# Moving the PSUM evacuations of the second attention layer behind the second exponential of a step on ScalarE

## The chip, the cores and the metric

The kernel runs on one core of one Trainium2 chip. The metric is device time in microseconds (us), the median of the runs shown. Five engines work side by side, each through its own instructions in order: PE (TensorE, matmuls; PEld is its loading of weights), DVE (VectorE), ACT (ScalarE), POOL (GpSimd) and SP (SyncE, which here only issues DMAs). They meet at semaphores. Matmuls write PSUM, and ACT or DVE carry the results from there to SBUF; that carrying is called evacuation below.

## What is computed

Four layers in float32 on x of shape (4, 1024, 256), each added to x after a layer norm: attention A (16 heads of 64), a feed-forward block (256 to 1024 to 256 with gelu), attention B, and the feed-forward block again. Cut to what matters, the third layer is:

```python
h = layernorm(layernorm(x)) * ln_scale + ln_bias
c_q, c_kv = h @ w_down_q.T, h @ w_down_kv.T          # 128 wide each
q, k, v = (c @ w_up.T for ...)                        # 16 heads of 64
q, k = rope(q), rope(k)
attn = softmax(q @ k.T / 8)
x = x + (attn @ v).reshape(b, s, 1024) @ w_out.T
```

## The kernel before, in words

The order of the work is written out by hand: each engine runs its instructions as the Python code issues them. An attention layer walks over 32 groups (four batches, eight pairs of heads) and over eight steps in each, 256 steps in all; a step is 128 query rows of one pair, 64 rows of each of two 64-row blocks, for both heads. `steps_with` (L339) is the loop over steps s. In step s it issues, for the step ahead, `scores(s+1)` (L247, PE, 16 matmul instructions into two tiles `sc`, one for each head), the negated maximum of each tile (L258, DVE), and two exponentials (L260, ACT, `exponentials(s+1, 0)` and `(s+1, 1)`). DVE then transposes the 32x32 squares of step s (L280), SP and POOL send the pieces to other partitions by DMA (L304), and ACT copies one piece (L296). Before that, `invert(s)` takes the reciprocal of the sums (L268, DVE) and copies it out (L269, ACT).

Two steps make one group of 128 query rows, h, five steps later (LAG): in a step with `part == 0`, called a *weighing step* here, PE multiplies the probabilities with v (`weigh`, L313, 128 matmul instructions, into two PSUM banks); ACT copies the two results (L323) and POOL scales them (L325). In the next step, `part == 1`, called a *projecting step* here, PE multiplies with the output weights (`project`, L176 with `wo,oT`), ACT evacuates (L335, `got`) and POOL adds to x (L337).

The work that prepares coming pairs is a table of pieces, each a step and a function. `(s - EARLY)` pieces stand between the two exponentials of step s, `s` pieces at its end. For attention B, `pair_b` gives for each pair two halves of q and k (`qk`: matmul and evacuation, L860), their rotation (`change` L865, `rotate` L870 to L872, a step and two steps later) and two halves of v (`values`, L881). They fall on projecting steps. In each pair two of the four projecting steps get one such piece, and two get two. `batch_b` adds for each coming batch, on some projecting steps that have one: four turnings of the normalized rows (`transposed`, L162 on PE, L167 on ACT) and four products with the down weights (`down`, L835).

PSUM has eight banks of 512 floats. The scores hold six of them: three tiles of two banks, taken in turn. All other results share the last two, which `group` hands out in turn:

```python
    def group(*shape):
        last[0] ^= 1
        return ps_mm.tile([P, *shape], F32, tag=f"m{last[0]}", name="mm")
```

So each new result waits until the one before the last has been evacuated, and the two banks of `weigh` are the banks that the projecting step before it used last. In a projecting step of attention B, ACT's order before the change is: `got` (L335), first exponential, evacuations of the pieces, second exponential. A projecting step with one piece takes two groups there, one with two pieces takes three.

Of the kernel before, what the change touches and what calls it, by code (L numbers as in the profile page):

```python
# [9 lines left out]
F32 = mybir.dt.float32  # L10
# [23 lines left out]
NK2 = S // DH  # L34
EPS = 1e-5
EARLY = 0.5
PLACES = {
    (3, 0): (0, 1), (3, 10): (2,), (3, 11): (3,), (3, 12): (4,), (3, 13): (5,),
    (3, 14): (6,), (3, 15): (7,), (3, 17): (8,), (3, 18): (9,), (3, 19): (14,), (3, 20): (15,),
    (4, 0): (16,), (4, 2): (10, 17), (4, 4): (18,), (4, 6): (19,), (4, 8): (20,), (4, 10): (21,),  # L40
    (4, 14): (11,), (4, 15): (22,), (5, 2): (12,), (5, 14): (13,), (5, 15): (23,),
    (6, 2): (26,), (6, 5): (27,), (6, 8): (28,), (6, 14): (24,), (6, 15): (25,),
    (7, 2): (29,), (7, 4): (30,), (7, 7): (31,), (7, 9): (32,), (7, 11): (33,), (7, 14): (38, 34),
    (7, 15): (35,), (7, 16): (39,), (7, 17): (36,), (7, 19): (37,),
}


# [1 line left out]
def hybrid_block_kernel(  # L49
# [137 lines left out]
                    start=(i == 0), stop=(i == len(parts) - 1),  # L187
                )

    def attention(prep_batch, prep_pair, wo, loader, lead, kept):  # L190

# [133 lines left out]
        def project(h):  # L327
            g, t0 = divmod(HB * h, NT)
            b, pr = pairs[g]
            po = group(HB, D)  # L330
            for t in range(HB):
                paired(po[:, t, :], [(oT[h][:, t], [wos[g][:, t]] * 2)])
            oT.pop(h)
            got = tmp.tile([P, HB, D], F32, tag="tmp", name="got")
            nc.scalar.copy(got, po)  # L335
            xd = xs[b][:, t0 : t0 + HB, :]
            nc.gpsimd.tensor_add(xd, xd, got)  # L337

        def steps_with(others):  # L339
            for k, f in others:  # L340
                pieces.setdefault(k, []).append(f)
            for s in range(-1, n + LAG + 1):
                h, part = divmod(s - LAG, HB)
                ahead = 0 <= s + 1 < n
                if 0 <= s < n:
                    invert(s)
                if ahead:
                    scores(s + 1)
                if part == 1 and 0 <= s // HB - 1 < n // HB:
                    send(s // HB - 1, nc.gpsimd, sent[len(sent) - POOL_DMA :])  # L350
                if part == 1 and 0 <= h < n // HB:
                    project(h)
                if ahead:
                    exponentials(s + 1, 0)
                for f in pieces.get(s - EARLY, ()):
                    f()
                if part == 0 and 0 <= h < n // HB:
                    weigh(h)
                if ahead:
                    exponentials(s + 1, 1)  # L360
                if part == 0 and 0 <= h < n // HB:
                    take(h)
                if 0 <= s < n:
                    turn(s)
                if part == 0 and 0 <= s // HB - 1 < n // HB:
                    keep(s // HB - 1)
                    T.pop(s // HB - 1)
                if part == 0 and 0 <= s < n:
                    send(s // HB, nc.sync, sent[: len(sent) - POOL_DMA])
                for f in pieces.get(s, ()):  # L370
                    f()
# [333 lines left out]
    def layer_a():  # L705
# [5 lines left out]
        def batch_a(b):  # L711
            work = []
            for qb in range(NQB):
                k = {}

                def straight(t, b=b, k=k, qb=qb):
                    if t == 0:
                        k["xn"] = xnp.tile([P, TQ, D], F32, tag="xn", name="xn")
                    dst, src = k["xn"][:, t, :], xs[b][:, qb * TQ + t, :]
                    shift, rstd = rows.factors(NQB * b + qb, t)[:2]  # L720
                    if b == 0 and qb == 1:
                        nc.vector.tensor_scalar(dst, src, rstd, shift, op0=ALU.mult, op1=ALU.add)
                    else:
                        standardize(dst, src, shift, rstd)

                def turned(c, b=b, k=k, qb=qb):
                    if c == 0:
                        p, tag = ((lowp, "low"), (highp, f"high{b % 2}"))[qb]
                        hTs[b, qb] = p.tile([P, NC, QB], F32, tag=tag, name="hT")
                    transposed(hTs[b, qb], k["xn"], c)  # L730

                work += [(10 * qb + t, lambda t=t, f=straight: f(t)) for t in range(TQ)]
                work += [(10 * qb + 6 + 2 * c, lambda c=c, f=turned: f(c)) for c in range(NC)]
            return work

        def pair_a(b, pr):
# [38 lines left out]

        later = [(4 + i, lambda i=i: rows.measure(2 + i // TQ, i % TQ)) for i in range(6 * TQ)]
        later += [(4 + 6 * TQ, lambda: rows.finish[2]())]
        first, steps = attention(batch_a, pair_a, wo_a, nc.gpsimd, lead=3, kept=0)
        loads, xn, pair = first[:2], first[2:14], first[14:]

        def measured(qb):
# [15 lines left out]
    def layer_b(rows):  # L797
# [4 lines left out]
        def batch_b(b):  # L802
            work = []
            for qb in range(NQB):
                k = {}

                def first(t, b=b, k=k, qb=qb):
                    if t == 0:
                        if b:
                            k["x1"] = xnp.tile([P, TQ, D], F32, tag="xn", name="x1")  # L810
                        else:
                            k["x1"] = vp.tile([P, NK2, DH], F32, tag="v", name="x1").rearrange(
                                "p k d -> p (k d)"
                            ).rearrange("p (t d) -> p t d", t=TQ)
                    xt = xs[b][:, qb * TQ + t, :]
                    standardize(k["x1"][:, t, :], xt, *rows.factors(NQB * b + qb, t)[:2])
                    nc.gpsimd.tensor_add(xt, xt, k["x1"][:, t, :])

                def second(t, b=b, k=k, qb=qb):
                    x1 = k["x1"][:, t, :]  # L820
                    nc.scalar.mul(x1, x1, rows.factors(NQB * b + qb, t)[2])

                def turned(c, b=b, k=k, qb=qb):
                    if c == 0:
                        p, tag = (highp, f"high{qb}") if b % 2 == 0 else (lowp, "low")
                        cs[b, qb] = p.tile([P, NC, QB], F32, tag=tag, name="hc")
                    transposed(cs[b, qb], k["x1"], c, affine=(lns_sb, lnb_sb))

                def down(m, b=b, qb=qb):

                    h = cs[b, qb][:, :, ts(m, QB // 2)]
                    pc = group(2, QB // 2)
                    for i in range(2):
                        paired(pc[:, i], [(wd_sb[:, i, c, :], [h[:, c]] * 2) for c in range(NC)])
                    nc.scalar.copy(h, pc)  # L835

                work += [(16 * qb - 14 + t, lambda t=t, f=first: f(t)) for t in range(TQ)]
                work += [(16 * qb - 12 + t, lambda t=t, f=second: f(t)) for t in range(TQ)]
                work += [(16 * qb - 8 + 2 * c - EARLY, lambda c=c, f=turned: f(c)) for c in range(NC)]
                work += [(16 * qb + 2 * m, lambda m=m, f=down: f(m)) for m in range(2)]  # L840
            return work

        def pair_b(b, pr):
# [6 lines left out]

            def qk(i, qb):

                pq = group(QB)
                paired(pq, [(made["w"][:, i, :], [cs[b, qb][:, i]] * 2)])
                name = ("qT", "kT")[i]
                if qb == 0:
                    made[name] = qkp.tile([P, S], F32, tag=name, name=name)
                straight = made[name][:, ts(qb, QB)]
                made[i, qb] = straight
                nc.scalar.mul(straight, pq, (scale_b, 1.0)[i])  # L860
# [13 lines left out]
            def values(qb):  # L874
                if qb == 0:
                    made["v"] = vp.tile([P, NK2, DH], F32, tag="v", name="v")
                pv = group(NK2 // NQB, DH)
                for t in range(NK2 // NQB):
                    lhsT = cs[b, qb][:, 1, ts(t, DH)]
                    by_head(pv[:, t, :], [(lhsT, made["w"][:, 2, :])])  # L880
                nc.scalar.copy(made["v"][:, ts(qb, NK2 // NQB), :], pv)  # L881

            work = []
            for i in (1, 0):
                for qb in range(NQB):
                    k = 2 - 4 * i + 2 * qb
                    work += [(k - EARLY, lambda i=i, qb=qb: qk(i, qb))]
                    work += [(k + 1, lambda i=i, qb=qb: change(i, qb))]
                    work += [(k + 2, lambda i=i, qb=qb: rotate(i, qb))]
            work += [(4 + 2 * qb - EARLY, lambda qb=qb: values(qb)) for qb in range(NQB)]  # L890
            return {name: lambda name=name: made[name] for name in ("qT", "kT", "v")}, load, work

        return attention(batch_b, pair_b, wo_b, nc.sync, lead=5, kept=1)


    n_steps = B * NF * NT
# [72 lines left out]
```

## Time and profile before

| what | value |
|---|---|
| median of 3 runs | 3253.63 us (3250.37 to 3256.33) |
| profiled execution | 3250.15 us |
| its span in the profile | 3248.4 us |
| busy over the span | PE 97%, PEld 64%, DVE 84%, ACT 66%, POOL 62% |
| granted TensorE clock | 0.996 |
| first to last transpose (L280) of attention B | 1671.8 to 3014.2 us |

Four stages follow one another: attention A up to about 1420 us, a feed-forward block up to about 1670, attention B up to about 3010, and the last feed-forward block. In attention B, from 2200 to 2400 us, PE is busy for 198.82 of 200 us, DVE 184.56, POOL 181.85 and ACT 155.75; the DMA engines have a busy share of 0.89.

The profile's tables are read like this. A line of the timeline has the start, the duration, the engine, the source line, the operation, output and inputs, the shapes and the count of merged instructions; in brackets stands the idle time before it and what ended it. A line of the waits has who waited for whom, the sum in us, the number of times and the longest.

### The profile page before, as it was taken

How to read it: one execution, taken by the hardware profiler on the slowest of the kernel's cores; microseconds unless marked ns; L12 is line 12 of the kernel's file. 1: busy time of each engine (PE TensorE's matmuls, PEld its weight loads, DVE VectorE, ACT ScalarE, POOL GpSimd, SP SyncE). 2: the span in 40 equal slices, each digit the busy share in tenths (PEclk: the TensorE clock that was granted, in tenths of full speed). 3: DMA queues.
4: the chain of work that ended last, by engine and by line, in shares of the span. 5: the costliest groups of instructions: out<-in, count | busy, mean ns of one | idle time of the engine just before them, and what ended most of it. 6: DMA issues, size and time to landing. Idle time of an engine off the chain costs nothing.

```text
span 3248.4 us, 128967 instructions
## 1 busy us (share of the span) xinstructions
PE 3164.4 (97%) x53648; PEld 2092.2 (64%) x53648; DVE 2723.5 (84%) x2686; ACT 2137.9 (66%) x4400; POOL 2002.1 (62%) x2782
## 2 busy tenths in 40 slices
PE   8999999999999999999999999999999999999999
PEld 4666666666666666668866566666666666655688
DVE  7988888888888888966569989998999999999554
ACT  5666666666666666655447777777778777777542
POOL 4544545455444545442249889899899889886311
PEclk9999999999999999999999999999999999999999
DMA  8888888888888888850029889988989899988200
GB/s 228 217 224 215 224 224 228 217 219 222 221 217 225 219 231 223 221 150 1 4 74 244 225 228 243 242 237 236 246 243 243 234 240 246 238 235 221 57 20 27
DMA packets 244709, 642.29 MB, mean 198 GB/s; under 512 B 74304, under 2 KB 102976, under 8 KB 244128
## 3 DMA queue, kind: packets, MB, share of 16 engines
q1 hardware_dynamic: 161104, 397.60, 48.0%
q0 software_dynamic: 83024, 236.44, 26.0%
q8 instruction: 426, 6.98, 1.0%
q14 instruction: 155, 1.27, 0.1%
HBM read 43.39 MB, written 4.19 MB: 15 GB/s over the span
## 4 chain that ended last, share of the span: by engine, by line
PE 69%; SPq 12%; DMA 6%; DVE 5%; ACT 4%; issue 3%; POOL 1%; DVEq 0%; ACTq 0%; POOLq 0%
PE sc L247 20%; PE mm L313 19%; PE mm L176 15%; SPq L304 11%; DMA pT<-T 5%; PE pw L495 4%; PE mm L185 4%; PE mm L495 3%; PE mm L615 2%; DVE T L280 2%; DVE nmax L258 1%; ACT p L260 1%; PE ph L604 1%; ACT gT L529 1%; PE mm L162 1%
## 5 line engine op out<-in xcount | busy, mean ns | idle before, releaser
L258 DVE TENSOR_REDUCE nmax<-sc 128x1 f32<-128x1024 f32 x1024 | 1204.5, 1218 | 214.3 <-PE sc L247 211.3
L260 ACT ACTIVATE p<-sc,nmax 128x1024 f32<-128x1024 f32 x1024 | 1145.3, 1119 | 322.3 <-DVE nmax L258 322.2
L280 DVE STREAM_TRANSPOSE T<-p 128x2176 f32<-128x2176 f32 x512 | 1247.3, 2436 | 48.4 <-DMA pT<-T 18.4
L247 PE MATMUL sc<-kT,qT 64*64 64x512 f32 x8192 | 1082.5, 598 | 11.9 <-ACT p L260 10.3
L313 PEld LDWEIGHTS mm<-pT,v 64*64 64x64 f32 x32768 | 949.5, 133 | 140.7 <-issue 98.5
L313 PE MATMUL mm<-pT,v 64*64 64x128 f32 x32768 | 983.0, 269 | 9.6 <-issue 8.5
L304 POOL DMA_DIRECT2D pT<-T x1280 | 629.6, 499 | 125.5 <-PE sc L247 57.7
L325 POOL TENSOR_TENSOR oT<-oT,pT 128x256 f32<-128x256 f32 x256 | 187.0, 730 | 696.3 <-ACT oT L323 623.0
L247 PEld LDWEIGHTS sc<-kT,qT 64*64 64x64 f32 x8192 | 332.8, 133 | 401.6 <-issue 274.5
L337 POOL TENSOR_TENSOR x<-x,got 128x512 f32<-128x512 f32 x256 | 331.0, 1293 | 25.8 <-ACT got L335 22.0
L335 ACT COPY got<-mm 128x512 f32<-128x512 f32 x256 | 150.0, 586 | 281.8 <-PE mm L176 281.8
L176 PE MATMUL mm<-wo,oT 128*64 128x256 f32 x2048 | 279.9, 394 | 24.1 <-POOL oT L325 22.8
L176 PEld LDWEIGHTS mm<-wo,oT 128*64 128x64 f32 x2048 | 124.9, 136 | 273.2 <-POOL oT L325 226.5
L269 ACT COPY p<-total 128x128 f32<-128x128 f32 x512 | 151.9, 297 | 198.6 <-DVE total L268 192.4
L176 PE MATMUL mm<-hT,w 128*64 128x512 f32 x1024 | 243.4, 597 | 0.9 <-ACT hT L165 0.9
L260 ACT ACTIVATION_READ_ACCUMULATOR p<-sc,nmax 128x1 f32 x1024 | 205.2, 200 | 0.0
L185 PEld LDWEIGHTS mm<-w,hT 128*64 128x64 f32 x4096 | 140.9, 138 | 71.3 <-issue 69.4
L871 POOL TENSOR_TENSOR turned<-turned,sin_sb 128x512 f32<-128x512 f32 x128 | 163.8, 1279 | 0.0
L409 POOL TENSOR_TENSOR x<-x,b_sb 128x256 f32<-128x256 f32 x64 | 48.8, 777 | 170.6 <-ACT xn L156 170.6
L296 ACT COPY pT<-T 32x1088 f32<-32x1088 f32 x128 | 140.3, 1096 | 4.9 <-DMA pT<-T 1.1
L185 PE MATMUL mm<-w,hT 128*64 128x64 f32 x4096 | 140.9, 222 | 0.2 <-ACT kT L758 0.2
L176 PEld LDWEIGHTS mm<-hT,w 128*64 128x64 f32 x1024 | 73.3, 138 | 96.8 <-issue 75.0
(145 smaller groups left out, 2928.5 us busy)
## 6 DMA issues: line engine op xcount, KB each, us to landing
pT<-T SPq DMA_DIRECT2D x2688, 136.0 KB, 4.7
pT<-T POOLq DMA_DIRECT2D x1280, 136.0 KB, 4.7
turned<-kT POOLq DMA_DIRECT2D x128, 128.0 KB, 3.4
turned<-qT POOLq DMA_DIRECT2D x128, 128.0 KB, 3.5
w<-in_wqkv_a POOLq DMA_DIRECT2D x96, 128.0 KB, 6.0
wo<-in_wo_a POOLq DMA_DIRECT2D x32, 128.0 KB, 5.4
wo<-in_wo_a POOLq DMA_DIRECT2D x64, 64.0 KB, 5.5
wo<-in_wo_b SPq DMA_DIRECT2D x32, 128.0 KB, 4.0
```

The source lines that it names most:

```text
L176: nc.tensor.matmul(out[ts(j, DH)], lhsT[:, ts(j, DH)], rhs[j], start=(first and i == 0), stop=(last and i == len(parts) - 1),)
L185: nc.tensor.matmul(out[ts(j, DH)], lhsT, rhs[:, ts(j, DH)], start=(i == 0), stop=(i == len(parts) - 1),)
L247: nc.tensor.matmul(sc[s, j][ts(half, DH), ts(m, 512)], qT()[rows, ts(2 * qs + half, DH)], kT()[rows, ts(m, 512)], start=True, stop=True,)
L258: nc.vector.tensor_reduce(nmax, sc[s, j], AX.X, ALU.max, negate=True)
L260: nc.scalar.activation(probs[s][:, :NK2, ts(j, 2), :], sc.pop((s, j)).rearrange("p (k c i) -> p k c i", c=2, i=SQ), AF.Exp, bias=nmax, acc ...
L280: nc.vector.transpose(T[h][:, :, q, :, :].rearrange("p c k i -> p k c i"), probs.pop(s))
L304: engine.dma_start(pT[h][ts(c, SQ), a], T[h][ts(a, SQ), c])
L313: nc.tensor.matmul(av[h][q][ts(j ^ q, DH)], v[ts(j, DH), k, :], pT[h][ts(j, DH), :, q, k, :], start=(k == 0), stop=(k == NK2 - 1),)
L325: nc.gpsimd.tensor_mul(parts, parts, pT.pop(h)[:, :, :, NK2, :])
L337: nc.gpsimd.tensor_add(xd, xd, got)
L495: nc.tensor.matmul(bank[:, t, : right(k).shape[-1]], left(t, k), right(k), start=(first and t == 0 and k == 0), stop=(k == n_k - 1), skip_ ...
L871: nc.gpsimd.tensor_mul(other, other, sin_sb[:, ts(qb, QB)])
```

## The change

Only attention B (`late=True`) changes. The functions that issue a matmul and its evacuation are cut in two: `qk` and `straightened`, `values` and `taken`; `project` hands back its evacuation `added`. The evacuations become pieces at `s - MIDDLE`, which run behind the second exponential. `added` also runs there, unless the pieces of the step that take a PSUM group (marked `banked`) are more than one; then it stays where it was. PLACES, the table that spreads the preparation of the first pair over the feed-forward block, gets the new numbers of the same pieces. The order of instructions on PE, DVE, POOL and SP stays the same; on ACT it changes.

```diff
+MIDDLE = 0.25
...
+    def banked(f):
+
+        f.banks = 1
+        return f
+
-    def attention(prep_batch, prep_pair, wo, loader, lead, kept):
+    def attention(prep_batch, prep_pair, wo, loader, lead, kept, late):
...
-            got = tmp.tile([P, HB, D], F32, tag="tmp", name="got")
-            nc.scalar.copy(got, po)
-            xd = xs[b][:, t0 : t0 + HB, :]
-            nc.gpsimd.tensor_add(xd, xd, got)
+
+            def added():
+                got = tmp.tile([P, HB, D], F32, tag="tmp", name="got")
+                nc.scalar.copy(got, po)
+                xd = xs[b][:, t0 : t0 + HB, :]
+                nc.gpsimd.tensor_add(xd, xd, got)
+
+            return added
...
                 if part == 1 and 0 <= h < n // HB:
-                    project(h)
+                    added = project(h)
+                    both = pieces.get(s - EARLY, []) + pieces.get(s, [])
+                    if not late or sum(getattr(f, "banks", 0) for f in both) > 1:
+                        added()
+                        added = None
...
                 if ahead:
                     exponentials(s + 1, 1)
+                if added:
+                    added()
                 if part == 0 and 0 <= h < n // HB:
                     take(h)
+                for f in pieces.get(s - MIDDLE, ()):
+                    f()
...
-                work += [(16 * qb - 8 + 2 * c - EARLY, lambda c=c, f=turned: f(c)) for c in range(NC)]
-                work += [(16 * qb + 2 * m, lambda m=m, f=down: f(m)) for m in range(2)]
+                work += [(16 * qb - 8 + 2 * c - EARLY, banked(lambda c=c, f=turned: f(c))) for c in range(NC)]
+                work += [(16 * qb + 2 * m, banked(lambda m=m, f=down: f(m))) for m in range(2)]
...
-                pq = group(QB)
+                pq = made["pq"] = group(QB)
                 paired(pq, [(made["w"][:, i, :], [cs[b, qb][:, i]] * 2)])
+
+            def straightened(i, qb):
+
+                pq = made["pq"]
                 name = ("qT", "kT")[i]
...
+            def taken(qb):
+
+                pv = made["pv"]
                 nc.scalar.copy(made["v"][:, ts(qb, NK2 // NQB), :], pv)
...
-                    work += [(k - EARLY, lambda i=i, qb=qb: qk(i, qb))]
+                    work += [(k - EARLY, banked(lambda i=i, qb=qb: qk(i, qb)))]
+                    work += [(k - MIDDLE, lambda i=i, qb=qb: straightened(i, qb))]
...
-            work += [(4 + 2 * qb - EARLY, lambda qb=qb: values(qb)) for qb in range(NQB)]
+            work += [(4 + 2 * qb - EARLY, banked(lambda qb=qb: values(qb))) for qb in range(NQB)]
+            work += [(4 + 2 * qb - MIDDLE, lambda qb=qb: taken(qb)) for qb in range(NQB)]
```

## The prediction, made before the result was known

> **What bounds the kernel now.** I read the page first: its slices show three regimes, and the change touches only attention B, 1672 to 3014 us. No engine is plainly the bound there (PE 99%, DVE 92%, POOL 91% of 2200 to 2400 us), so shares do not decide.
>
> ```profile
> PE 3164.4 (97%) x53648; PEld 2092.2 (64%) x53648; DVE 2723.5 (84%) x2686; ACT 2137.9 (66%) x4400; POOL 2002.1 (62%) x2782
> ```
>
> ACT, the engine whose order changes, is idle a third of the span. It matters only through who waits for it. From the list of waits, 1800 to 2900 us:
>
> ```profile
> ACT got L335 <- PE mm L176: 106.8, 105, 3.8
> ...
> PEld sc L247 <- ACT p L260: 34.8, 47, 3.4
> ...
> DVE total L268 <- ACT p L260: 20.6, 48, 4.0
> ```
>
> ACT stands still 106.8 us waiting for the projection, with the first exponential queued behind; PE waits 34.8 us for exponentials, to get score tiles back, and DVE 20.6 us for the second one. These are the waits the change can remove. What ends last is seen in the timeline of PE for two steady rounds, a projecting step with three PSUM groups (from 1962.79) and one with two (from 1972.80):
>
> ```profile
> 1962.79 1.08 PE L176 MATMUL mm<-wo,oT 128*64 128x256 f32 x8
> ...
> 1965.62 2.04 PE L247 MATMUL sc<-kT,qT 64*64 64x512 f32 x16
> 1967.39 3.76 PE L313 MATMUL mm<-pT,v 64*64 64x128 f32 x127
> ...
> 1974.67 2.57 PE L247 MATMUL sc<-kT,qT 64*64 64x512 f32 x13
> ...
> 1977.50 2.75 PE L313 MATMUL mm<-pT,v 64*64 64x128 f32 x92
> ```
>
> In the first round PE has no hole: projection, two pieces, scores, then weighing 1.77 us after the scores began. In the second there is one: scores begin at 1974.67, but all but two of their matmuls wait until 1975.73, when the first exponential has given its tile back; weighing starts in earnest 1.77 later, at 1977.50. Both rounds last 10.01 us from `got` to `got`. So the three-group round is bound by PE's own stream, and the two-group round by projection, `got`, exponential, scores, weighing. Now ACT and DVE in the same rounds:
>
> ```profile
> 1963.97 0.59 ACT L335 COPY got<-mm 128x512 f32<-128x512 f32 x1 [0.94 <-PE mm L176]
> 1964.45 1.12 ACT L260 ACTIVATE p<-sc,nmax 128x1024 f32<-128x1024 f32 x1
> ...
> 1965.56 0.59 ACT L881 COPY v<-mm 128x512 f32<-128x512 f32 x1
> 1966.02 0.62 ACT L860 ACTIVATE kT<-mm 128x512 f32<-128x512 f32 x1
> ...
> 1973.99 0.59 ACT L335 COPY got<-mm 128x512 f32<-128x512 f32 x1 [0.94 <-PE mm L176]
> 1974.47 1.12 ACT L260 ACTIVATE p<-sc,nmax 128x1024 f32<-128x1024 f32 x1
> ```
>
> ```profile
> 1972.91 2.36 DVE L258 TENSOR_REDUCE nmax<-sc 128x1 f32<-128x1024 f32 x2 [0.31 <-PE sc L247]
> ```
>
> The evacuations of a step are done by 1966.64, before PE reaches the weighing at 1967.39. That is the margin the change spends: weighing writes the same two banks.
>
> **The change, part by part.** It adds and removes no work; only ACT's order moves. Durations: an exponential occupies ACT 1.10 to 1.11 us (1964.45 to 1965.56), an evacuation 0.47 when another follows, 0.59 to 0.62 to its end, and PE resumes 0.05 after ACT's end. The exponential can start 1.25 us after its maximum starts (1967.85 to 1969.11 one step later).
>
> *Three groups (60 of the 124 rounds between 1700 and 2990 us).* `got` stays ahead, so the first exponential keeps 1964.45. The second follows at 1965.56 (its maximum has been there since 1965.2), v at 1966.67, k at 1967.14, done at 1967.76. Weighing writes the first piece's bank and, from its third matmul, the last piece's: it waits until 1967.80. Before, it ran freely from 1967.46 (its last matmul's start, 1970.88, less the 3.42 that an unhindered weighing takes from first to last start). The loss is +0.34 us, and the same in every such round, since all of them follow `got` at the same distances. 60 x 0.34 = **+20 us**. Queued on PE behind weighing are the next scores, and behind these DVE's maxima: nothing catches up, since the next round is tight as well.
>
> *Two groups, no further piece (37 rounds).* Now `got` goes behind. The first exponential can start at 1972.91 + 1.25 = 1974.16 instead of 1974.47: scores resume 0.3 earlier and weighing could start at 1977.2. But second exponential 1975.3 (just behind its maximum), `got` 1976.4, k 1976.9, done 1977.47: the banks are free at 1977.52, against 1977.50. Gain and wait cancel: +0.07 at most in 25 quiet rounds, +1.7. In the 12 rounds where the projection comes late (its input waits for POOL), the exponentials no longer wait for it: by each round's own lateness, 0.05 to 1.04, together -5.5. Sum **-4 us**.
>
> *Two groups and a turning (12).* `got` stays ahead; the turning's evacuation L167 keeps its place between the exponentials (0.67), and the moved one stands behind all. In the round of 2223.14: first exponential 2223.62, turning 2224.73, second exponential 2225.40, k from 2226.5 to 2227.1; weighing, whose last matmul started 3.4 us after a start near 2226.6, begins 0.5 later. 12 x 0.53 = **+6 us**.
>
> *Two groups and a product with the down weights (12).* Its evacuation was behind the second exponential already, PE's product takes 1.87 us more: **0**. *Projection alone (3 at the end):* 0.3 earlier each, **-1**.
>
> DVE's wait for the second exponential (20.6 us) goes, since that is now 0.5 to 1.0 us earlier; but DVE is next late for PE's scores (DVE nmax L258 waited 43.9 us for them), and these start later. I count it as nothing; bounds 0 to -20. POOL's add waits for the later `got`, in two-group rounds until 1977.0 instead of 1976.24; behind it are three rotations (3.8 us) and the scaling of oT, which waited 0.53 us for a DMA at 1981.87. So the cover is about that long; below it 0, without it 0.75 x 37 = +28. I take 0. The rotation's DMA (POOL L865) reads the moved k or q, in place 1.3 us later, at 1977.47; it is issued at 1982.54, behind the scaling. SP's sends (L304) do not move in their queue.
>
> A rule weighed: the Trainium skill, "Perfetto Trace Analysis", section Optimizing Tensor Performance (Matmuls), wants independent matmul groups to rotate through different banks, so that one's evacuation overlaps the next one's matmuls. With two banks for groups the trace bears it out only while evacuations end 0.75 us ahead of PE, as at 1966.64; the change ends them behind it. By the rule alone the 37 two-group rounds would lose like the others, 37 x 0.34 = 13 us, and the sum would be +38 us; by the rows it is the one below.
>
> Sum: 20 - 4 + 6 - 1 = +21. In about a fifth of the rounds (25 of 124) the projection is late because POOL is busy, and a late weighing before it costs nothing: off a fifth, -4. So +17 on the profiled 3250.15 us is 3267; the median of the runs stands 3.5 above that execution, and I forecast **3270 us**.
>
> **The rivals.**
>
> *A, the exponentials win, faster.* If ACT's chain is some 0.35 us shorter than reckoned, or weighing is mostly held by something else, the banks are free in time. Then two-group rounds gain the whole 0.29 (37 x 0.29 = 11), the late ones some 5 more, DVE's waits bring a little: -15, 3239 us. For it: the 34.8 and 20.6 us above. Against it: three-group rounds have nothing to gain at all. It decides where the last evacuation ends before scores start + 1.77.
>
> *B, hidden, no change.* SP is almost never idle (20 sends took 18.25 us from 1952.52 on, loads of weights most of the rest of two rounds), and the DMA share is 0.89 to 0.91. If the DMAs set the mean pace (10.4 us a round, against 10.01 when quiet), the longer rounds only use up slack: 3254 us. Against it: DVE waited for DMAs to free T for only some 20 us.
>
> *C, POOL becomes the bound, slower still.* The later `got` pushes rotations, scaling and the next projection. Half of the 28 us above would add 14: 3284 us. For it: POOL at 91%. Against it: it waits for DMA or ACT ahead of the scaling in most quiet rounds.
>
> That the order does not change as described is excluded: built, the kernels differ on ACT alone.
>
> **How the numbers follow.** Forecast 0.54, A 0.17, B 0.17, C 0.12. What a measurement can tell from no change is about 0.2%, 3247 to 3260. Slower: forecast and C, 0.66; same: B, 0.17; faster: A, 0.17. The range runs from 3245 (B with the DVE waits gone, and the upper part of A) to 3290 (C and the 28 us in part); it leaves out most of A and a little of C.
>
> **What would show it.** In the profile after: three-group rounds with 10.3 us from one first exponential to the next; PE's weight load for weighing (L313 of before) waiting for an evacuation of k, q or v, some 0.3 us each and 25 us in all, a wait that does not exist now; DVE's wait for the second exponential gone; its wait for scores grown. I am wrong if weighing keeps its 1.77 us after the scores in three-group rounds, or if quiet rounds are no longer the rule, so that SP's or POOL's queue sets the pace.

## The result, and the profile after

The changed kernel takes 3269.73 us (median of 9 runs, 3262.99 to 3278.52), the kernel before 3253.63 (9 runs beside them, 3250.37 to 3262.66): a ratio of 1.0048, with a 95% interval of 1.0038 to 1.0058. It is slower by 16 us. The profiled execution of the changed kernel took 3269.71 us, its span is 3267.9 and its granted clock 0.996, as before, so the two traces may be laid side by side.

The line of busy times from the page of the changed kernel:

```profile
PE 3184.2 (97%) x53648; PEld 2125.9 (65%) x53648; DVE 2718.8 (83%) x2686; ACT 2146.6 (66%) x4400; POOL 2000.6 (61%) x2782
```

The work is the same, instruction for instruction. PE's busy time grew by 20 us, which means only that its matmuls stand open longer while something waits. What waits is in the list of waits of the changed kernel, 1800 to 2900 us (who for whom, sum in us, times, longest):

```profile
DVE nmax L264 <- PE sc L253: 101.4, 120, 4.1
...
ACT got L343 <- PE mm L177: 78.7, 76, 3.1
...
POOL x L345 <- ACT got L343: 24.7, 26, 1.3
PEld sc L253 <- ACT p L266: 21.8, 39, 3.6
PEld mm L319 <- ACT qT L883: 20.8, 32, 1.2
...
PEld mm L319 <- ACT got L343: 15.0, 28, 0.6
...
PEld mm L319 <- ACT v L908: 12.8, 25, 0.5
...
PEld mm L319 <- ACT kT L883: 7.2, 6, 1.2
...
DVE total L274 <- ACT p L266: 2.4, 2, 1.6
```

All that the change was made for did happen: ACT waits 28 us less for the projection (106.8 before), PE 13 us less for exponentials (34.8), DVE 18 us less for the second one (20.6). In their place stand four lines that the list of before does not have at L313: weighing (L319 now) waits for q, v, k and `got`, 55.8 us together. And DVE waits 101.4 us for scores, where it waited 43.9, and ACT 128.3 us for DVE's maxima, where it waited 96.5.

The timeline of PE for the same kind of rounds as in the prediction, a three-group round from 1968.62 and a two-group round from 1978.98:

```profile
1968.62 1.08 PE L177 MATMUL mm<-wo,oT 128*64 128x256 f32 x8
...
1971.46 2.04 PE L253 MATMUL sc<-kT,qT 64*64 64x512 f32 x16
1973.22 4.00 PE L319 MATMUL mm<-pT,v 64*64 64x128 f32 x126
...
1978.98 1.08 PE L177 MATMUL mm<-wo,oT 128*64 128x256 f32 x8
...
1980.85 2.71 PE L253 MATMUL sc<-kT,qT 64*64 64x512 f32 x16
1983.23 4.10 PE L319 MATMUL mm<-pT,v 64*64 64x128 f32 x126
```

And ACT in these rounds:

```profile
1969.81 0.59 ACT L343 COPY got<-mm 128x512 f32<-128x512 f32 x1 [1.02 <-PE mm L177]
1970.29 1.12 ACT L266 ACTIVATE p<-sc,nmax 128x1024 f32<-128x1024 f32 x1
...
1971.39 1.11 ACT L266 ACTIVATE p<-sc,nmax 128x1024 f32<-128x1024 f32 x1
...
1972.48 0.59 ACT L908 COPY v<-mm 128x512 f32<-128x512 f32 x1
1972.94 0.62 ACT L883 ACTIVATE kT<-mm 128x512 f32<-128x512 f32 x1
...
1980.37 1.11 ACT L266 ACTIVATE p<-sc,nmax 128x1024 f32<-128x1024 f32 x1 [1.22 <-DVE nmax L264]
...
1982.60 0.57 ACT L343 COPY got<-mm 128x512 f32<-128x512 f32 x1
1983.06 0.61 ACT L883 ACTIVATE kT<-mm 128x512 f32<-128x512 f32 x1
```

Read the first round like this: the two matmuls of weighing that open it (each is two instructions in the profile) start at 1973.22, still 1.76 behind the scores, but they write the bank of v, free at 1973.07. The third writes the bank of k, and that is evacuated at 1972.94 + 0.62 = 1973.56; its first instruction starts at 1973.62. So the group's duration of 4.00 (3.76 before) has a hole in it that the list shows only as a wait of the weight load. This round's `got` starts 10.35 us after that of the round before it (1959.46), where 10.01 us lay between two of them. In the second round `got` and k end at 1983.17 and 1983.67, and weighing starts its first matmuls at 1983.23 and the rest behind k: the exponential came early and nothing of it is left.

All 127 rounds of attention B, from the start of weighing's last matmul to that of the next, sorted by what stands in them (worked out from the two traces, one execution each):

| kind of round | count | quiet (median) before, after | sum before, after | difference |
|---|---|---|---|---|
| three groups | 60 | 10.02, 10.36 | 619.8, 637.2 | +17.4 |
| two groups | 37 | 10.07, 10.10 | 386.1, 381.0 | -5.1 |
| turning | 12 | 10.02, 10.86 | 122.0, 132.5 | +10.5 |
| down product | 12 | 10.79, 10.79 | 138.5, 134.3 | -4.2 |
| alone, and ends | 6 | | 67.6, 67.0 | -0.6 |
| sum | 127 | | | +18.0 |

The profiled executions differ by 3269.71 - 3250.15 = 19.6 us, so 18 of them lie in these rounds. The quiet rounds and the sums of three-group rounds and turnings are steady, the other sums are not: another profiled execution of the changed kernel (3280.25 us, from the experiments) has 636.4 us in three-group rounds, 132.3 in those with a turning, but 389.4 in two-group rounds.

### The profile page after: what moved, and what is told of

It is laid out like the page before. It is cut to its first block, busy times and chain, and to the rows that moved or that the text cites. A ratio compares the mean times of both kernels' runs of the same rounds, so it can differ in the third digit from the quotient of the medians.

```text
span 3267.9 us, 128967 instructions
## 1 busy us (share of the span) xinstructions
PE 3184.2 (97%) x53648; PEld 2125.9 (65%) x53648; DVE 2718.8 (83%) x2686; ACT 2146.6 (66%) x4400; POOL 2000.6 (61%) x2782
## 4 chain that ended last, share of the span: by engine, by line
PE 68%; SPq 14%; DMA 7%; ACT 4%; DVE 3%; issue 3%; POOL 1%; ACTq 0%; DVEq 0%; POOLq 0%
PE sc L253 19%; PE mm L319 19%; PE mm L177 14%; SPq L310 13%; DMA pT<-T 6%; PE mm L186 4%; PE pw L514 4%; PE mm L514 3%; PE mm L634 2%; ACT p L266 1%; PE ph L623 1%; DVE T L286 1%; POOL oT L331 1%; DVE nmax L264 1%; ACT gT L548 1%
## 5 line engine op out<-in xcount | busy, mean ns | idle before, releaser
L253 PE MATMUL sc<-kT,qT 64*64 64x512 f32 x8192 | 1065.6, 598 | 11.5 <-ACT p L266 8.7
L319 PEld LDWEIGHTS mm<-pT,v 64*64 64x64 f32 x32768 | 952.5, 133 | 175.3 <-issue 60.3
L319 PE MATMUL mm<-pT,v 64*64 64x128 f32 x32768 | 1000.9, 270 | 19.5 <-issue 12.5
L253 PEld LDWEIGHTS sc<-kT,qT 64*64 64x64 f32 x8192 | 365.6, 133 | 364.2 <-issue 229.2
L345 POOL TENSOR_TENSOR x<-x,got 128x512 f32<-128x512 f32 x256 | 330.1, 1290 | 62.3 <-ACT got L343 58.7
```

What stands on the lines that cost most here:

```text
L253: nc.tensor.matmul(sc[s, j][ts(half, DH), ts(m, 512)], qT()[rows, ts(2 * qs + half, DH)], kT()[rows, ts(m, 512)], start=True, stop=True,)
L319: nc.tensor.matmul(av[h][q][ts(j ^ q, DH)], v[ts(j, DH), k, :], pT[h][ts(j, DH), :, q, k, :], start=(k == 0), stop=(k == NK2 - 1),)
```

## The experiments

Two theories stood against each other. The **bank theory**, that of the forecast: a round gets longer when its last evacuation on ACT ends after PE has come to the weighing that writes the same banks; the 60 three-group rounds and 12 turnings pay, the two-group rounds come out even. The **POOL theory**, rival C: the later `got` delays POOL's addition, and with it rotations, scaling and the next projection; then it is the two-group rounds, the only ones in which `got` moved, that pay. Later a second question came up, where a gain goes that quiet rounds show and the whole kernel does not.

All ratios are to the kernel before, run between the others on the same chip; its median was 3258.62 us in the first sitting (e1 to e4), 3255.93 in the second (e5 to e8) and 3254.32 in the third (e9 to e12). A ratio is not the quotient of the two medians; they differ by up to 0.0008. In the experiments' code, `place` says where the projection's evacuation stands in a projecting step of attention B: 0 at the front, 1 behind the first exponential, 2 behind the second. `tails` are evacuations of q, k and v that are put behind the second exponential. `banks` counts the step's pieces that take a PSUM group.

### One half of the change alone: two-group rounds

```diff
+                place = (2 if banks <= 1 else 0) if late else 0
...
+                    if late and banks <= 1 and getattr(f, "split", None):
+                        tails.append(f.split())
+                    else:
+                        f()
```

> The evacuations stand behind the second exponential only in the rounds that take two PSUM groups; rounds with three groups (two pieces, a turning or a down product beside the projection) keep the order of before. Bank theory (weighing is held by the moved evacuations of three-group rounds and rounds with a turning): those rounds fall back to 10.0 us, the two-group rounds keep their small gain of about 5 us, so 3246 to 3251 us, ratio 0.998 to 1.000. Rival POOL theory (the loss comes from the projection's result reaching POOL later, which happens in two-group rounds alone): the loss stays, 3266 to 3272 us, ratio 1.004 to 1.006.

Measured: 3255.74 us, 1.0 within the interval (0.9999, 0.9987 to 1.0011). The half in which `got` moves costs nothing, so the POOL theory falls. (The execution that was profiled took 3266.13 us, 10 above the median, so sums over its rounds are not compared; its quiet two-group round has 10.16 us, its three-group round is back at 10.06.)

### The other half: rounds with more groups

```diff
+                place = (0) if late else 0
...
+                    if late and banks > 1 and getattr(f, "split", None):
+                        tails.append(f.split())
+                    else:
+                        f()
```

> The other half: the projection's evacuation always stands ahead as before, the pieces' evacuations move behind the second exponential only in rounds with three groups. Bank theory: the whole loss and none of the gain of the two-group rounds, 3271 to 3282 us, ratio 1.0055 to 1.0085. POOL theory: nothing is lost, 3250 to 3257 us, ratio 0.999 to 1.001.

Measured: 3268.13 us, 1.0026 (1.0016 to 1.0037). Slower, as the bank theory has it, and in the right rounds: three groups 10.36 us, turnings 10.87, two groups 10.01. But the ratio is less than half of what I expected. A part of that is the kernel before, which ran 5 us longer in this sitting; for the rest the half and the whole were measured side by side.

### The whole and this half once more, side by side

No edit: the changed kernel and the half above, in one sitting.

> The changed kernel once more, beside the kernel before and the three-group half on the same chip, since the two halves did not add up to the whole (0.9999 and 1.0026 against 1.0048, from different sittings). If the gap is the sitting's: the ratio comes out near 1.003 like that of the three-group half. If the two-group half really costs something once three-group rounds are longer: 1.0045 to 1.0055 again, 5 to 8 us above the three-group half.

> The three-group half once more, for the same comparison. Bank theory with a fifth hidden: 1.006; with half hidden, as the first measurement has it: 1.0025 to 1.0035.

Measured: the changed kernel 3272.71 us, 1.0050 (1.0036 to 1.0064); the half 3268.34 us, 1.0039 (1.0026 to 1.0052). The half carries most of the loss, and the two intervals overlap; its ratio lies between the two values that were reckoned. In the traces the bank theory's rounds cost the same in the half and in the whole: three-group rounds 635.3 and 638.6 us in the two executions of the half, 637.2 and 636.4 in those of the whole, turnings between 132.0 and 132.5. Whether the two-group half, which costs nothing alone, takes another 4 us when the three-group rounds are long already stays open: two sittings point that way and neither shows it.

### A spare 0.54 us on ACT, ahead of the evacuations or behind them

If the end of the last evacuation sets the round, time put on ACT ahead of it must show in the round, and the same time behind it must not. Two copies into an unused 128x128 tile, in the projecting steps with two pieces, in one kernel ahead of the deferred evacuations and in the other behind them:

```diff
+                if late and sum(hasattr(f, "pair") for f in pieces.get(s - MIDDLE, ())) > 1:
+                    nc.scalar.copy(spare, ident)
+                    nc.scalar.copy(spare, ident)
                 for f in pieces.get(s - MIDDLE, ()):
                     f()
```

> The changed kernel with two extra ACT copies of 128x128 (about 0.40 us the two) between the second exponential and the evacuations, in the 61 rounds with two pieces. Nothing reads them. Bank theory: the last evacuation ends 0.40 us later in each of these rounds and PE's weighing with it, 60 x 0.40 = 24 us less a fifth that is hidden: 19 to 25 us above the changed kernel, 3288 to 3296 us, ratio 1.0105 to 1.013. Rival (the loss has nothing to do with when these evacuations end): at most a few us above, ratio 1.004 to 1.007.

> The same two extra copies, in the same rounds, but just behind the evacuations. ACT has the same work as with the copies ahead; the banks come free when they do in the changed kernel. Bank theory: ACT waits 0.8 to 1.0 us for the next maximum there anyway, so 0 to 4 us above the changed kernel, ratio 1.004 to 1.0065. Rival (ACT's load as such delays its exponentials): as much as with the copies ahead.

Measured: ahead 3295.4 us, 1.0112 (1.0098 to 1.0125); behind 3273.72 us, 1.0047 (1.0033 to 1.006), the same as the changed kernel without them. ACT in the kernel with the copies ahead:

```profile
1966.38 0.30 ACT L386 COPY spare<-ident 128x128 f32<-128x128 f32 x1
1966.72 0.30 ACT L387 COPY spare<-ident 128x128 f32<-128x128 f32 x1
1966.92 0.59 ACT L891 ACTIVATE qT<-mm 128x512 f32<-128x512 f32 x1
```

and PE there:

```profile
1965.43 1.97 PE L258 MATMUL sc<-kT,qT 64*64 64x512 f32 x16
1967.57 4.08 PE L324 MATMUL mm<-pT,v 64*64 64x128 f32 x126 [0.17 <-ACT qT L891]
```

The pair of copies pushes q from 1966.38 to 1966.92, by 0.54 us, and weighing, 1.76 behind the scores in the changed kernel, is now 2.14 behind them and waits for q: 1966.92 + 0.59 = 1967.51, and the matmul starts at 1967.57. The quiet three-group round grows from 10.36 to 10.89, by 0.53. So the delay goes into the round one to one, and the same copies behind the evacuations leave it at 10.36. Both kernels load ACT alike. **This shows the mechanism**: what counts is where in ACT's order the evacuation ends, not how much ACT does, as long as ACT has idle time there (0.96 us ahead of the next exponential in the round of the changed kernel shown above). Over the whole kernel 21.7 us of 61 x 0.54 = 33 arrive at the medians. In the two traces the three-group rounds alone take 27.9 us more (666.8 against 638.9); where the rest stays was not followed.

### Better than both? The projection's evacuation behind the first exponential

In the two-group rounds of before, the first exponential stands 0.3 us behind `got`, and the pieces' evacuation has a margin. So `got` goes between the first exponential and the piece, and everything else stays as it was before:

```diff
+                place = (1 if banks <= 1 else 0) if late else 0
...
                 if ahead:
                     exponentials(s + 1, 0)
+                if added and place == 1:
+                    added()
```

> Attention B only, rounds with two PSUM groups: the projection's evacuation stands between the first exponential and the piece's evacuation; all else as before the change. The first exponential no longer waits for the projection, and the banks are free 0.8 us before PE wants them. Bank theory: the 0.29 us of each quiet two-group round is gained (37 x 0.29 = 11 us) and some 5 us in rounds with a late projection; a third may be lost again to DMA waits: 3240 to 3248 us against 3254, ratio 0.995 to 0.998. Rival (the first exponential does not bind these rounds, or SP and the DMAs do): 0.999 to 1.001.

Measured: 3250.97 us, 0.9987 (0.9978 to 0.9995). Of the kernels that leave nothing out this is the fastest, but the gain is 5 us on the medians where I expected 6 to 16; the ratio lies just outside both theories' ranges, between them. PE and ACT in one of its two-group rounds:

```profile
2309.98 1.08 PE L176 MATMUL mm<-wo,oT 128*64 128x256 f32 x8
...
2311.85 2.27 PE L252 MATMUL sc<-kT,qT 64*64 64x512 f32 x13
...
2314.37 3.34 PE L318 MATMUL mm<-pT,v 64*64 64x128 f32 x115
```

```profile
2311.35 1.11 ACT L265 ACTIVATE p<-sc,nmax 128x1024 f32<-128x1024 f32 x1 [0.84 <-DVE nmax L263]
...
2312.45 0.57 ACT L342 COPY got<-mm 128x512 f32<-128x512 f32 x1
2312.92 0.61 ACT L884 ACTIVATE kT<-mm 128x512 f32<-128x512 f32 x1
```

Both evacuations end by 2313.53, ahead of the bulk of weighing at 2314.37, and that stands 4.39 us behind the projection's start where it stood 1977.50 - 1972.80 = 4.70 behind it. The quiet two-group round falls from 10.07 to 9.75 us, about the gain of a freed exponential. In these two traces, one execution each, the two-group rounds give 10.9 us in sum. But the three-group rounds, in which nothing was changed, take 13.1 us more (632.9 against 619.8; their median 10.12 against 10.02). The next kernel has the same attention B, and its trace says the same (375.8 and 632.0 us). So one kind of round gives back what another gains: all of it in these traces, about half of it at the medians, where 5 us of 37 x 0.33 = 12 arrive. It goes with late projections. Let one be called late when it starts more than 0.15 us later than in a quiet round, reckoned from the last score matmul ahead of it (the last three of the layer, which have none, are left out): 40 are late before, by 25.5 us together, and 56 here, by 37 us.

### The same order in attention A

```diff
-        first, steps = attention(batch_a, pair_a, wo_a, nc.gpsimd, lead=3, kept=0, late=False)
+        first, steps = attention(batch_a, pair_a, wo_a, nc.gpsimd, lead=3, kept=0, late=True)
```

> The same order in attention A too. There every round takes three groups, PE has no hole, and the matmuls of the values (third group) need the projection's bank: at 807.82 us in the trace of before, while the moved evacuation would end at about 805.31 + 2.95 = 808.26. Bank theory: 0.4 us lost in some 120 rounds of attention A, 45 to 55 us above the kernel that moves it in attention B alone, ratio 1.009 to 1.014. Rival (freeing the first exponential is good wherever it waits): faster still, below 0.995.

Measured: 3312.14 us, 1.0166 (1.0153 to 1.018); 61 us over the kernel above. Attention A's last transpose ends at 1485.4 instead of 1424.0 us (before), so all of it lies there. Waits of this kernel, 200 to 1400 us:

```profile
PEld mm L185 <- ACT got L342: 123.5, 105, 1.2
...
PE mm L185 <- ACT got L342: 31.6, 101, 0.3
```

In the kernel before, the first of these is 0.3 us, once, and the second is not there.

In attention A the third group of a projecting step is issued right behind the second, ahead of the scores, and it takes the bank of the first, that of the projection. In the kernel before, PE gets there 2.63 us after the projection's start (797.07 after 794.44). Now `got` stands behind an exponential, and with the projection at 802.36 PE starts that group 3.11 us later:

```profile
805.47 1.15 PE L185 MATMUL mm<-w,hT 128*64 128x64 f32 x32 [0.31 <-ACT got L342]
```

From 802.36 to the next projection, 813.64, it is 11.28 us; in the trace of before such a round (794.44 to 805.19) has 10.75. So 0.48 of the 0.53 lie in front of this group; 0.53 x the 105 rounds of the list is 56 us. The same move gains in one layer and loses in the other, by who takes the bank next. The direction was as expected; the loss was larger than expected.

### Who takes the gain back: POOL without one addition

The rotation's second product needs an addition on POOL (L872 of before, 1.28 us each). Without it POOL has some 155 us less work in 1290 (121 additions of 1.28 us), and what its queue hides or gives back must change. The three kernels leave out the rotation's sum.

```diff
-                nc.gpsimd.tensor_add(straight, straight, other)
```

> The kernel before without the third POOL instruction of the rotation (the sum of the two products is left out, so q and k are not rotated rightly; 1.27 us of POOL in each round). It is the base for the next two kernels. If POOL's queue is what makes the projection late (22.5 of 37 us of lateness in the trace of before stood behind a busy POOL): 8 to 22 us faster than before, ratio 0.993 to 0.9975. If the DMAs are: 0.998 to 1.000.

> The changed kernel without the same instruction (the rotation's sum is left out). Bank theory, with POOL's lateness as what hid part of the loss: against the kernel before without the add it loses more than the 16 us of the full kernels, 60 x 0.34 + 12 x 0.84 = 30 less 5: 20 to 30 us, difference of the ratios 0.006 to 0.009. If the DMAs hide it: 12 to 18 us again, 0.004 to 0.0055.

> The order with the projection's evacuation between the first exponential and the piece, in two-group rounds of attention B, without the same instruction (the rotation's sum is left out). In the full kernel its quiet two-group rounds fell from 10.07 to 9.75 us, 11 us in all, and three-group rounds grew by as much. If POOL's lateness gave it back: now 10 to 16 us faster than the kernel before without the add, difference of the ratios 0.003 to 0.005. If the DMAs did: 0 to 5 us, below 0.0015.

Measured: before without it 3244.14 us (0.9963, 0.9951 to 0.9975), changed without it 3257.84 (1.0013, 1.0004 to 1.0022), `got` between without it 3238.52 (0.9953, 0.9941 to 0.9965). The first ratio lies in the range for POOL's queue as what makes projections late: they are late by 13 us together where it was 25.5. The change costs 0.0050 with a lighter POOL too, as it does in the full kernel (0.0048 and 0.0050), so POOL's queue hides no part of it that these intervals can show (0.0015 either way, 5 us). And `got` between gains 0.0010, with 0.0017 either way, where the full POOL had 0.0013: that POOL's queue takes the whole gain back (0.003 to 0.005 was reckoned for it) is not borne out. **A part is not excluded**: in these traces, one execution each, the two-group rounds give 8.3 us (388.3 to 380.0) and the three-group rounds take 4.2 more (618.4 to 622.6), not 13.1, and lateness grows by 3 us, not by 11. What the lighter POOL waits for is seen in the waits of before without the addition, 1700 to 2990 us:

```profile
POOL oT L325 <- ACT oT L323: 244.0, 117, 5.5
```

(38.5 us in the kernel before.) The scaling of oT now mostly stands ready for ACT's copy, and yet the kernel is only 10 us faster.

### SP and the DMAs: one send more on SP

```diff
+        pool_dma = 4 if late else 5
```

With `got` between, one of the five pieces that POOL sends in each group of attention B goes to SP's queue.

> The same order, complete, with one of POOL's five sends of a round in attention B moved to SP (4 on POOL, 11 on SP): POOL is 0.49 us lighter in each round, SP 0.6 to 0.8 us heavier. If POOL's queue gave the gain back: faster than the order alone, ratio 0.993 to 0.997. If SP's queue and the DMAs set the mean pace: slower, 1.001 to 1.01.

Measured: 3263.29 us, 1.0029 (1.0019 to 1.004): 0.0042 slower than the same kernel with five sends on POOL, which ran in the sitting before. POOL is relieved and the kernel loses 12 to 14 us, so work on SP's side costs. The waits say through whom: POOL's scaling waits 71.5 us for pieces that a DMA brings (51.6 with five sends), and DVE 33.9 us for DMAs to read T (16.5). That execution took 3254.55 us, the fastest of the ten, so these sums are rather too small. It speaks for SP's queue or the DMA engines as a part of what sets the mean pace, 10.4 us a round where quiet ones have 10.0. Which of the two, and whether POOL and DVE, busy 91 and 92% from 2200 to 2400 us in the trace of before, have a part, stays open.

## Why the forecast was right, step by step

- **Three groups, +20 us.** Right in mechanism and size. The quiet round grew by 0.34 (10.02 to 10.36), as worked out from the order on ACT; k ends 3.75 us after the start of `got`, where 3.79 was reckoned. The sum, +17.4, holds already what the prediction took off apart for late projections. That 0.34 fits so closely is the balance of two small things that the working left out: two matmuls go ahead of the wait, and the rest then starts from a standstill (see the turnings).
- **Two groups, -4 us.** Right in mechanism: quiet rounds +0.03 (reckoned +0.07 at most), since the exponentials are early and the banks are late by as much. The sum, -5.1, comes from one execution of each kernel and is not steady (another has +3.3); that the two-group half alone does nothing to the time is measured (0.9999, with 4 us either way).
- **Turning, +6 us.** The mechanism is right and the size was not: 0.84 a round, 10.5 in sum. Here weighing's first matmul waits, and PE stands still, where in three-group rounds two matmuls go ahead. These lines of PE in the changed kernel show it:

```profile
2164.98 3.92 PE L319 MATMUL mm<-pT,v 64*64 64x128 f32 x125 [0.31 <-ACT qT L883]
...
2168.70 0.31 PE L319 MATMUL mm<-pT,v 64*64 64x128 f32 x3
```

q is out at 2164.93. From the first start to the last, near 2168.74, it is 3.76 us, where an unhindered weighing takes 3.42: these 0.3 us, the price of starting from a standstill, are the missing part of the term. Its first three instructions start 0.16 us apart (2164.98, 2165.14, 2165.30).
- **Down product, 0.** The quiet round is the same (10.79). The sum is 4.2 us less in these two executions; together with the turnings' 4.5 too many it cancels. That the forecast is off by less than 1 us is luck of this kind: the profiled executions differ by 19.6 us where 17 were reckoned, and the medians by 16.1.
- **A fifth hidden, -4 us.** The bearing is right, the size too small. By their quiet rounds the kinds would have grown by 60 x 0.34 + 12 x 0.84 + 37 x 0.03 = 32 us, and they grew by 18: 14 us were hidden, where the prediction took off 9.5 (4 here, 5.5 in late two-group rounds). Late projections, counted as above, were 40 before, by 25.5 us (the prediction's 25 are those that it put down to a busy POOL), and are 18 after, by 16 (22 and 17 in the other execution). That the longer rounds let POOL and the DMAs catch up fits this, and was not tested by itself.
- **DVE's wait for the second exponential, 0.** Right: 18 us of it went, and its wait for scores grew by 57. DVE is fed by PE, and PE was late.
- **POOL's addition, 0 (to +28).** POOL did wait 24.7 us for `got`, near the upper bound. The time did not: the two-group half alone costs nothing, and the change costs as much with a lighter POOL, within 5 us.
- **Rival A (3239).** Fails by its own condition: the last evacuation ends 0.34 after scores + 1.77 in three-group rounds. **Rival B** (3254) was wrong, but what it named exists: of the 32 us by which quiet rounds grew, 16 arrived at the medians. **Rival C** is measured away.
- **The signs.** Three-group rounds were to take 10.3 us and take 10.36. The weight load's waits for q, v and k were to be 25 us and are 40.8, since a weight load starts to wait ahead of its matmul (0.5 us each, of which PE loses 0.34, and 1.2 in turned rounds, of which it loses 0.84).

The rule that was weighed, of the Trainium skill, "Perfetto Trace Analysis", section Optimizing Tensor Performance (Matmuls), has independent groups rotate through banks so that an evacuation overlaps the next group's matmuls. Taken alone, as the prediction did, it would have had the 37 two-group rounds lose 0.34 us each, 13 us. The trace decides against that part: their quiet rounds grew by 0.03 us, since the exponential's earlier start pays for the late bank.

## What to carry to other kernels

Where all banks of a rotation are in use, note for each evacuation when it ends and when PE writes that bank next; an evacuation that is moved behind other work of its in-order engine costs what it ends late by in every quiet round, however idle the engine is on average. Put it behind the one instruction that others wait for, and no further: behind the first exponential it kept its margin in attention B, and in attention A, where PE takes that bank sooner, even that cost 61 us. And do not expect quiet rounds to add up to the whole: here 16 of 32 us of loss and 5 of 12 us of gain arrived at the medians, since longer rounds had fewer late projections and shorter ones more. Look for what the rounds with no change in them do.

## What the runs showed of the hardware

A weighing that starts from a standstill, behind a semaphore, takes 3.76 us from its first matmul's start to its last, where one that follows other matmuls takes 3.42. Two ACT copies of 128x128, shown as 0.30 us each, hold up the next instruction by 0.54 us together. SP's sends of probabilities, all of 136 KB, occupy its queue between 0.51 and 1.53 us each (5th to 95th percentile, median 0.60, in the kernel before, 1700 to 2990 us): its sends took 996 of these 1290 us, so an engine with no line among the busy ones, since issuing DMAs is not counted there, was among the fullest.
